# A message-passing layer: destination terms made window by window on the core instead of read back from a table in memory

## The chip, the cores and the metric

The kernel runs on one core of one Trainium2 chip. The core has a matrix engine (TensorE, PE in the profile, its weight loads PEld), a vector engine (VectorE, DVE), an activation engine (ScalarE, ACT), a programmable engine (GpSimd, POOL) and a queue engine that here only starts transfers (SyncE, SP). The metric is device microseconds for one execution, lower is better. "Group" below is 384 edges, "block" is four groups.

## The reference, cut to what matters

There are 12500 nodes with 64 features and 212500 edges with 32 features. The edges are sorted by destination.

```python
msg_in = concat([nodes[src], nodes[dst], edge_features])       # 212500 x 160
messages = relu(msg_in @ mW1 + mb1) @ mW2 + mb2                # hidden width 128
aggregated = segment_sum(messages, dst)                        # 12500 x 64
update = relu(concat([nodes, aggregated]) @ uW1 + ub1) @ uW2 + ub2
out = layernorm(nodes + update)
```

Since `mW1` acts on three parts, the hidden layer of an edge is a sum of three terms: source features, edge features, and a destination term `nodes[dst] @ mW1[64:128] + mb1` that depends on the destination alone.

## The kernel before, in words

All of it is float32. Edges go through in G = 554 groups of three tiles of 128 edges. The order of each engine's instructions is the order in which the program writes them (`manual_schedule`); the framework adds the semaphores. Because the edges are sorted, the destinations of one group lie within a window of W = 32 nodes that begins at the group's first destination. A flag checks on the chip that this holds; another routine (`unordered`, untouched, not run here) stands behind it.

What is kept on the core: `xc`, 65 partitions by 12544 columns (row 0 counts the edges of each node, rows 1 to 64 are the node features, transposed), and `agg`, the sum of hidden vectors by node.

For iteration g the main loop (L402 to L416) writes this:

- `inputs` (L257), every fourth group: SP loads the edge features of four groups into `st`.
- `gather(g + 16)` (L93): three indirect transfers by GpSimd, each 128 rows of source features, into one of 18 buffers `s`. The buffer of group g + 16 is that of group g - 2, so the gather waits until `sums(g - 2)` has read it.
- `tables_for(g + 8)` (L191): when its time has come, one `table()` (L180): up to four products of 128 columns of `xc` with `w1b` (the destination part of `mW1` and `mb1`) on PE, one ScalarE copy from PSUM, and one transfer of 256 KB to the table `by_dst` in memory. There are 25 of these.
- `window(g + 4)` (L269): SP reads 32 rows of `by_dst` from the group's first destination into the top 32 rows of `wm`, one of six right-hand sides of 128 x 128; the rest of `wm` holds the source and edge parts of `mW1`, loaded once. Every fourth group it first loads four starting columns into registers of SP and DVE.
- `onehot(g + 2)` (L282): DVE writes the one-hot of each edge's place in the window beside the gathered features.
- `turn(g + 1)` (L290): PE transposes three tiles of one-hot and features into `xt`; ScalarE copies them into `st` and sums the one-hots into `counts`.
- `hidden(g)` (L302): PE multiplies three tiles of `st` by `wm` into `pre`; ScalarE takes the relu into `h`. The one-hot rows pick the destination term out of the window.
- `sums(g - 2)` (L317): PE transposes the counts and multiplies `h` by the one-hots into `sg`, one of two PSUM buffers; a product is written four times over so that it is wide enough.
- a step of a pending node update (L385), four steps for every 512 nodes.
- `add(g - 2)` (L328): DVE adds `sg` into the window's columns of `agg`, and the counts into row 0 of `xc`, at columns held in a register.

Each engine takes its own share of this list in order. So DVE's order is one-hot of g + 2, then the update's steps, then the two additions of g - 2; PE's is transposes of g + 1, products of g, sums of g - 2. PSUM's eight banks are all given out: one for the iota, one for tables and updates, two each for `xt`, `pre` and `sg`.

The start-up clamps the first destinations to a plan of which table chunks are ready (`bound`, two sets of some 25 small fills on DVE).

Of the kernel before, what the change touches and what calls it, by code (L numbers as in the profile page):

```python
# [10 lines left out]
F32 = mybir.dt.float32  # L11
BF16 = mybir.dt.bfloat16
I32 = mybir.dt.int32
AF = mybir.ActivationFunctionType
ALU = mybir.AluOpType
ET = mybir.EngineType
PSUM = bass.MemoryType.PSUM
DRAM = bass.MemoryType.DRAM

P = 128  # L20
N = 12500
E = 212500
D = 64
DE = 32
H = 128
# [3 lines left out]
W = 32  # L29
TG = 3  # L30
GE = TG * P
G = (E + GE - 1) // GE
SB = 4
AHEAD = 16
NEXT = 4
NT = (E + P - 1) // P
NP = N + 44
CH = 512
TIMES = 4
# [8 lines left out]
def plan():  # L48


    import math

    def node(g, sign):
        q = min(1.0, g * GE / E)
        return g * GE * N / E + sign * (6.0 * math.sqrt((E - N) * q * (1 - q)) * N / E + 6)

    chunks, b = [], 0
    for e in [c * CH for c in range(1, N // CH + 1)] + [N]:
        opens = next((g for g in range(G) if node(g, 1) + W >= b), G)
        closes = next((g for g in range(G) if node(g, -1) >= e), G)  # L60
        n = e - b
        chunks.append((b, *((P, n // P) if n % P == 0 else (n // 2, 2)), opens, closes))
        b = e
    return chunks


PLAN = plan()
# [3 lines left out]
def ordered(ctx: ExitStack, tc: tile.TileContext, a, ok):  # L71
# [3 lines left out]
    nc = tc.nc  # L75
    x, out = a["x"], a["out"]
    const = ctx.enter_context(tc.tile_pool(name="const", bufs=1))
    dram = ctx.enter_context(tc.tile_pool(name="dram", bufs=1, space=DRAM))
    gp = ctx.enter_context(tc.tile_pool(name="gather", bufs=AHEAD + 2))
    stp = ctx.enter_context(tc.tile_pool(name="st", bufs=3))  # L80
    bp = ctx.enter_context(tc.tile_pool(name="bout", bufs=2))
# [30 lines left out]
    ones = const.tile([P, P], F32, name="ones")  # L112
# [3 lines left out]
    zero = const.tile([W, H], F32, name="zero")  # L116
# [5 lines left out]
    xc = const.tile([D + 1, NP], F32, name="xc")  # L122
# [4 lines left out]
    nc.sync.dma_start(xc[0:1, :].rearrange("o (p n) -> o p n", p=P), ones[:, : NP // P])  # L127
    w1b = const.tile([D + 1, H], F32, name="w1b")
    nc.scalar.dma_start(w1b[0:1, :], a["mb1"][None, :])
    nc.scalar.dma_start(w1b[1 : D + 1, :], a["mW1"][D : 2 * D, :])  # L130
    cuts = [0, 3 * CH, 12 * CH, N]
# [3 lines left out]
    NW = 6  # L135
# [9 lines left out]

    lo, hi = np.zeros(G), np.full(G, float(N - 1))
    for base, p, n, opens, closes in PLAN:
        lo[closes:] = base + p * n
        hi[:opens] = np.minimum(hi[:opens], base - W)

    def steps(v):

        at = [0, *(np.flatnonzero(np.diff(v)) + 1).tolist(), len(v)]
        return [(i, j, float(v[i])) for i, j in zip(at, at[1:])]

    bound = temp.tile([1, G], F32, name="bound")

    def set_bound(v):
        for i, j, value in steps(v):
            nc.vector.memset(bound[:, i:j], value)  # L160

    set_bound(hi)
    start_f = temp.tile([1, G], F32, name="start_f")
    nc.vector.tensor_scalar(start_f, first_f[0:1, :], 0.0, None, ALU.max)
    nc.vector.tensor_tensor(start_f, start_f, bound, ALU.min)
# [8 lines left out]


    by_dst = dram.tile([N + W, H], F32, name="by_dst")
    nc.sync.dma_start(by_dst[N:, :], zero)
    tables = list(PLAN)

    def table():  # L180
        base, p, n, _, _ = tables.pop(0)
        ps = ups.tile([H, CH], F32, name="u_ps").rearrange("p (n h) -> p n h", n=4)
        for k in range(n):
            nc.tensor.matmul(ps[:p, k], xc[:, base + k : base + p * n : n], w1b,  # L184
                             start=True, stop=True)
        t = bp.tile([P, 4, H], F32, name="t")
        nc.scalar.activation(t[:p, :n], ps[:p, :n], AF.Copy)  # L187
        nc.scalar.dma_start(
            by_dst[base : base + p * n, :].rearrange("(p n) h -> p n h", p=p), t[:p, :n])

    def tables_for(g):  # L191

        while tables and tables[0][3] <= g:
            table()

    SOON = NEXT + 4
    tables_for(SOON)


# [17 lines left out]
    nc.tensor.matmul(wps[:, 2, 0:1], u1s, b2, start=True, stop=True)  # L217
# [3 lines left out]

    nc.vector.tensor_tensor(ub1, ub1, wps[:, 2, 0:1], ALU.subtract)
# [8 lines left out]
    wrong = temp.tile([1, 2, G], F32, name="wrong")  # L231
    nc.vector.tensor_tensor(wrong[:, 0], first_f[0:1, :], bound, ALU.is_gt)
    set_bound(lo)
    nc.vector.tensor_tensor(wrong[:, 1], first_f[0:1, :], bound, ALU.is_lt)
    nwrong = temp.tile([1, 1], F32, name="nwrong")
    nc.vector.tensor_reduce(nwrong, wrong, mybir.AxisListType.XY, ALU.add)
# [18 lines left out]
    st, starts, hs = {}, {}, {}  # L255
# [13 lines left out]
    def window(g):  # L269
        if g >= G:  # L270
            return
        if g % SB == 0:
            n = min(SB, G - g)
            _, v = nc.values_load_multi_w_load_instructions(
                start_i[0:1, g : g + n], engines=[ET.SP, ET.DVE], min_val=0, max_val=N - 1,
                skip_runtime_bounds_check_because="they were clamped to the nodes on the chip",
            )
            for i in range(n):
                starts[g + i] = v[i]
        nc.sync.dma_start(wm[g % NW][:W, :], by_dst[bass.ds(starts[g], W), :])  # L280

# [35 lines left out]
    def sums(g):  # L317
        h, s = hs.pop(g), gathered.pop(g)
        sizes = tiles_of(g)
        sg = sgp.tile([P, TIMES + 1, W], F32, name="sg")  # L320
        nc.tensor.transpose(sg[0:1, TIMES, :], counts[:W, g : g + 1], ident[:W, :W])  # L321
        for j, p in enumerate(sizes):
            nc.tensor.matmul(sg[:, :TIMES, :], h[:p, j, :],  # L323
                             s[:p, j, :W].unsqueeze(1).to_broadcast([p, TIMES, W]),
                             start=j == 0, stop=j == len(sizes) - 1)
        return sg
# [6 lines left out]
    def update(base, p, n):  # L333
# [8 lines left out]
        def first(xin):  # L342
            u_ps = ups.tile([H, CH], F32, name="u_ps")
            nc.tensor.matmul(u_ps[:, :q], wc, agg[:, rows], start=True, stop=False)  # L344
            nc.tensor.matmul(u_ps[:, :q], ux, xc[:, rows], start=False, stop=True)  # L345
            u = up.tile([H, CH], F32, name="u")
            nc.scalar.activation(u[:, :q], u_ps[:, :q], AF.Relu, bias=ub1)
            nc.vector.tensor_tensor(xin[:p, :n], xin[:p, :n],
                                    u2b[:p].unsqueeze(1).to_broadcast([p, n, D]), ALU.add)
            return xin, u  # L350
# [31 lines left out]
    waiting = [(closes, update(base, p, n)) for base, p, n, _, closes in PLAN]  # L382
# [14 lines left out]
    for g in range(NEXT):  # L397
        window(g)
# [3 lines left out]
    for g in range(G + 2):  # L402
        if g < G:
            if g % SB == 0:
                inputs(g // SB + 2)
            if g + AHEAD < G:
                gather(g + AHEAD)
            tables_for(g + SOON)
            window(g + NEXT)
            onehot(g + 2)  # L410
            turn(g + 1)
            hidden(g)
        if g > 1:
            sg = sums(g - 2)
            step_update(g - 2)
            add(g - 2, sg)  # L416
# [331 lines left out]
```

## Time and profile before

| | |
|---|---|
| median of three runs | 2540.38 us (2536.92 to 2542.14) |
| the profiled execution, its time | 2528.93 us |
| its span, first to last instruction | 2527.2 us |
| PE, PEld busy | 1697.3 us (67%), 1457.9 us (58%) |
| POOL busy | 1570.3 us (62%) |
| ACT, DVE busy | 598.2 us (24%), 392.9 us (16%) |
| mean granted clock of TensorE | 0.786 |
| transfers from `by_dst`, to `by_dst` | 554 of 16 KB on SP's queue, 25 on ACT's |

The profile shows one execution. A line of groups reads: source line, engine, operation, output and inputs by the program's names, shape, count; then busy time and the mean of one in nanoseconds; then the idle time of that engine just before them and what ended most of it. In the timeline the columns are start and duration in microseconds, the engine, the line, the operation, its tiles, how many were merged, and in square brackets the idle time before it with what ended it. "remote" is a wait whose end the profile can't lay to an instruction. Ends of matmuls are modelled, so the better sign that a product is finished is the moment at which an engine that was waiting for it starts.

### The profile page before, as it was taken

To read this page: it belongs to the slowest core of one execution; us is meant where nothing else is said; L and a number is where in the kernel's file an instruction comes from. 1 tells how busy PE (TensorE), PEld (TensorE's weight loads), DVE (VectorE), ACT (ScalarE), POOL (GpSimd) and SP (SyncE) were. 2 spreads that over 40 slices of the span, in tenths; PEclk is the share of its full clock that TensorE was granted. 3 is DMA by queue.
4 is the path that set the end of the run, shared out by engine and by line. 5 is a ranking of instruction groups with operands and counts; after the bars stand their busy time and mean duration, and the time that the engine had idled before them with its cause. 6 is when DMAs were issued, how large, how long until landed. Compare 5 with 4: busy or idle time off the path is not lost.

```text
span 2527.2 us, 31410 instructions
## 1 busy us (share of the span) xinstructions
PE 1697.3 (67%) x9359; PEld 1457.9 (58%) x9359; DVE 392.9 (16%) x2103; ACT 598.2 (24%) x1740; POOL 1570.3 (62%) x1668
## 2 busy tenths in 40 slices
PE   0566767776676776776666766666667676677667
PEld 0455656665565665665555655556566565666556
DVE  3111111111111111111111111111111111111112
ACT  0222222222222222222222222222222222222223
POOL 6666666666666666666666665666666666666661
PEclk9787777777778677777877787788787778787879
DMA  5111111111111111111111111111111111111111
GB/s 127 34 43 46 40 43 45 41 44 43 40 44 41 42 47 39 45 43 40 43 41 42 47 42 40 40 43 44 41 42 47 36 47 40 43 47 38 46 39 28
DMA packets 99895, 111.48 MB, mean 44 GB/s; under 512 B 39997, under 2 KB 65062, under 8 KB 99590
## 3 DMA queue, kind: packets, MB, share of 16 engines
q0 software_dynamic: 53152, 54.51, 9.6%
q1 hardware_dynamic: 41928, 45.07, 6.4%
q10 hardware_dynamic: 4638, 9.80, 1.3%
q8 instruction: 79, 1.29, 0.2%
q14 instruction: 98, 0.80, 0.1%
HBM read 99.55 MB, written 9.62 MB: 43 GB/s over the span
## 4 chain that ended last, share of the span: by engine, by line
PE 66%; another core or an unknown queue 16%; issue 12%; DVE 2%; ACT 1%; DVEq 0%; DMA 0%; ACTq 0%
PE sg L323 25%; PE pre L307 21%; PE xt L298 12%; PE sg L321 2%; PE u_ps L184 2%; PE u_ps L357 2%; PE u_ps L344 1%; PE u_ps L345 1%; ACT st L299 1%; DVE o L374 0%; DVE mv L364 0%; DVE stats L363 0%; DVE xc L331 0%; DVE y L359 0%
## 5 line engine op out<-in xcount | busy, mean ns | idle before, releaser
L97 POOL DMA_INDIRECT s<-in_x,src_sb x1661 | 1569.6, 945 | 910.3 <-issue 420.5
L307 PE MATMUL pre<-wm,st 128*128 128x128 f32 x3322 | 635.3, 343 | 205.1 <-issue 140.3
L307 PEld LDWEIGHTS pre<-wm,st 128*128 128x128 f32 x3322 | 572.1, 254 | 241.7 <-issue 165.3
L323 PE MATMUL sg<-s,h 128*128 128x128 f32 x3322 | 660.4, 348 | 1.8 <-issue 1.8
L298 PE MATMUL xt<-ident,s 128*96 128x128 f32 x1661 | 355.4, 335 | 443.8 <-remote 246.7
L323 PEld LDWEIGHTS sg<-s,h 128*128 128x128 f32 x3322 | 535.6, 240 | 29.2 <-issue 1.7
L298 PEld LDWEIGHTS xt<-ident,s 128*96 128x96 f32 x1661 | 234.3, 159 | 501.7 <-remote 259.2
L299 ACT ACTIVATE st<-xt 96x384 f32<-96x384 f32 x554 | 267.9, 484 | 1002.3 <-PE xt L298 469.4
L311 ACT ACTIVATE h<-pre 128x384 f32<-128x384 f32 x553 | 268.8, 486 | 668.0 <-PE pre L307 257.3
L330 DVE TENSOR_TENSOR agg<-sg,agg 128x32 f32 x554 | 106.2, 192 | 1899.2 <-PE sg L323 761.2
L285 DVE TENSOR_TENSOR s<-iota,dlc 128x96 f32<-128x96 f32 x554 | 141.9, 257 | 54.6 <-issue 53.7
L184 PE MATMUL u_ps<-w1b,xc 65*128 65x128 f32 (+1 forms) x196 | 54.2, 453 | 112.9 <-DVE xc L331 80.3
L184 PEld LDWEIGHTS u_ps<-w1b,xc 65*128 65x128 f32 (+1 forms) x196 | 47.5, 326 | 118.2 <-issue 51.9
L321 PE MATMUL sg<-ident,counts 32*1 32x32 f32 x554 | 107.2, 194 | 0.0
L299 ACT ACTIVATION_READ_ACCUMULATOR st<-xt 96x1 f32 x554 | 106.0, 191 | 0.0
L331 DVE TENSOR_TENSOR xc<-sg,xc 1x32 f32 x554 | 99.2, 179 | 13.9 <-PE u_ps L345 5.3
L321 PEld LDWEIGHTS sg<-ident,counts 32*1 32x1 f32 x554 | 41.1, 74 | 90.2 <-issue 43.9
L357 PE MATMUL u_ps<-u,u 128*128 128x64 f32 (+1 forms) x196 | 49.5, 399 | 20.5 <-issue 11.2
L357 PEld LDWEIGHTS u_ps<-u,u 128*128 128x128 f32 (+1 forms) x196 | 47.1, 324 | 23.2 <-issue 12.2
L344 PE MATMUL u_ps<-agg,wc 128*128 128x512 f32 (+1 forms) x50 | 33.3, 753 | 18.0 <-DVE agg L330 12.2
L187 ACT ACTIVATE t<-u_ps 128x512 f32<-128x512 f32 (+1 forms) x25 | 14.7, 588 | 91.3 <-issue 43.7
L366 ACT ACTIVATE rstd<-mv,eps 128x4 f32<-128x4 f32 (+1 forms) x25 | 7.4, 297 | 103.8 <-DVE mv L364 42.1
(51 smaller groups left out, 188.1 us busy)
## 6 DMA issues: line engine op xcount, KB each, us to landing
s<-in_x,src_sb POOLq DMA_INDIRECT x1661
st<-in_efT SPq DMA_DIRECT2D x138, 192.0 KB
wm<-by_dst SPq DMA_DIRECT2D x554, 16.0 KB
by_dst<-t ACTq DMA_DIRECT2D x24, 256.0 KB
xin<-in_x SPq DMA_DIRECT2D x24, 128.0 KB
out<-o SPq DMA_DIRECT2D x24, 128.0 KB
xc<-in_xT ACTq DMA_DIRECT2D x1, 1589.0 KB
xc<-in_xT ACTq DMA_DIRECT2D x1, 1152.0 KB
```

The lines of the kernel that those rows point to most:

```text
L97: nc.gpsimd.indirect_dma_start(out=s[:p, j, W:], out_offset=None, in_=x[:, :], in_offset=bass.IndirectOffsetOnAxis(ap=src_sb[:p, t : t + 1 ...
L184: nc.tensor.matmul(ps[:p, k], xc[:, base + k : base + p * n : n], w1b, start=True, stop=True)
L285: nc.vector.tensor_tensor(gathered[g][:, :, :W], iota.unsqueeze(1).to_broadcast([P, TG, W]), dlc[:, g * TG : (g + 1) * TG].unsqueeze(2).to ...
L298: nc.tensor.transpose(xt[:, j * P : j * P + p], s[:p, j, :], ident[:p, :p])
L299: nc.scalar.activation(t[: D + W, c : c + n], xt[:, :n], AF.Copy, accum_out=counts[:, g : g + 1])
L307: nc.tensor.matmul(pre[:p, j, :], t[:, c + j * P : c + j * P + p], wm[g % NW], start=True, stop=True)
L311: nc.scalar.activation(h, pre, AF.Relu)
L321: nc.tensor.transpose(sg[0:1, TIMES, :], counts[:W, g : g + 1], ident[:W, :W])
L323: nc.tensor.matmul(sg[:, :TIMES, :], h[:p, j, :], s[:p, j, :W].unsqueeze(1).to_broadcast([p, TIMES, W]), start=j == 0, stop=j == len(sizes ...
L330: nc.vector.tensor_tensor(agg[:, at], sg[:, 0, :], agg[:, at], ALU.add)
L331: nc.vector.tensor_tensor(xc[0:1, at], sg[0:1, TIMES, :], xc[0:1, at], ALU.add)
L357: nc.tensor.matmul(o_ps[:p, k], u[:, k:q:n], u2, start=True, stop=True)
```

## The change

The table `by_dst`, its products, its copies and its transfers are gone, and with them the plan of ready chunks. `xc` gets a row of ones (row 65), so that `mb1` is its last row in `w1b`; row 0, the counts, meets a row of zeros. Once per block, `places` (written at iterations 1, 5, 9, ...) loads the four starting columns into DVE's registers and copies four windows of 66 partitions by 32 columns out of `xc` into `xw`, side by side. `windows` (written inside `sums` of the first group of a block, that is at iterations 2, 6, 10, ...) makes one product on PE, 128 window rows by 128, for the next block; it goes into 128 more columns of the same PSUM tile `sg` into which that `sums` then writes, and DVE copies its four parts of 32 rows by 128 columns into the top rows of four of now eight `wm`. Everything else in the loop stays.

```diff
-    xc = const.tile([D + 1, NP], F32, name="xc")
+    xc = const.tile([D + 2, NP], F32, name="xc")
+    nc.vector.memset(xc[:, N:], 0.0)
...
-    nc.sync.dma_start(xc[0:1, :].rearrange("o (p n) -> o p n", p=P), ones[:, : NP // P])
+    nc.sync.dma_start(xc[0:1, :].rearrange("o (p n) -> o p n", p=P), zero)
+    nc.sync.dma_start(xc[D + 1 :, :].rearrange("o (p n) -> o p n", p=P), ones[:, : NP // P])
...
-    NW = 6
+    NW = 2 * SB
...
-    def table():
-        base, p, n, _, _ = tables.pop(0)
-        ps = ups.tile([H, CH], F32, name="u_ps").rearrange("p (n h) -> p n h", n=4)
-        for k in range(n):
-            nc.tensor.matmul(ps[:p, k], xc[:, base + k : base + p * n : n], w1b,
-                             start=True, stop=True)
-        t = bp.tile([P, 4, H], F32, name="t")
-        nc.scalar.activation(t[:p, :n], ps[:p, :n], AF.Copy)
-        nc.scalar.dma_start(
-            by_dst[base : base + p * n, :].rearrange("(p n) h -> p n h", p=p), t[:p, :n])
...
-    def window(g):
...
-        nc.sync.dma_start(wm[g % NW][:W, :], by_dst[bass.ds(starts[g], W), :])
+    def places(b):
+
+        g, n = b * SB, min(SB, G - b * SB)
+        if n <= 0:
             return
+        _, v = nc.values_load_multi_w_load_instructions(
+            start_i[0:1, g : g + n], engines=[ET.DVE], min_val=0, max_val=N - 1,
+            skip_runtime_bounds_check_because="they were clamped to the nodes on the chip",
+        )
+        xw = xwp.tile([D + 2, SB, W], F32, name="xw")
+        for i in range(n):
+            starts[g + i] = v[i]
+            nc.vector.tensor_copy(xw[:, i, :], xc[:, bass.ds(v[i], W)])
+        xws[b] = xw, n
+
+    def windows(b, wp):
+
+        if b not in xws:
+            return
+        xw, n = xws.pop(b)
+        nc.tensor.matmul(wp[: n * W, :], xw[:, :n, :], w1b, start=True, stop=True)
+        for i in range(n):
+            nc.vector.tensor_copy(wm[(b * SB + i) % NW][:W, :], wp[i * W : (i + 1) * W, :])
...
     def sums(g):
...
-        sg = sgp.tile([P, TIMES + 1, W], F32, name="sg")
+        sgw = sgp.tile([P, (TIMES + 1) * W + H], F32, name="sg")
+        sg = sgw[:, : (TIMES + 1) * W].rearrange("p (t w) -> p t w", w=W)
+        if g % SB == 0:
+            windows(g // SB + 1, sgw[:, (TIMES + 1) * W :])
...
-    for g in range(NEXT):
-        window(g)
+    places(0)
+    windows(0, ups.tile([H, CH], F32, name="u_ps")[:, :H])
...
-            tables_for(g + SOON)
-            window(g + NEXT)
+            if g % SB == 1:
+                places(g // SB + 1)
             onehot(g + 2)
             turn(g + 1)
             hidden(g)
```

## The prediction

> **What bounds the kernel now.** I read the table of engines first, and it does not settle it: PE is busy 67% of the span and POOL 62%. The groups by line and POOL's waits settle it.
>
> ```profile
> L97 POOL DMA_INDIRECT s<-in_x,src_sb x1661 | 1569.6, 945 | 910.3 <-issue 420.5
> ```
>
> ```profile
> POOL s L97 <- issue: 420.5, 1376, 0.6
> POOL s L97 <- DVE agg L330: 301.7, 152, 8.2
> POOL s L97 <- remote: 68.6, 38, 2.6
> POOL s L97 <- PE sg L323: 59.9, 40, 3.1
> POOL s L97 <- PE pre L307: 25.2, 27, 4.3
> POOL s L97 <- PE xt L298: 17.9, 13, 3.6
> ```
>
> The gathers take 1569.6 us busy and 910.3 us of idle time before them, 2480 us of a span of 2527 us: POOL is never long without a gather, and what follows its last one is 47 us. A gather takes 0.945 us and 0.31 us (420.5 / 1376) to the next, so 1.25 us, 3.75 us for a group's three, 15.0 us for a block. The rest are pauses in which the next buffer is not yet read out: the last five rows, 473 us in 270 pauses, 1.75 us each, one for every 2.05 groups, 3.4 us in each of 139 blocks.
>
> Two stretches of the timeline say why it pauses although PE is not full. First with gathers running:
>
> ```profile
> 1203.77 0.50 PE L298 MATMUL xt<-ident,s 128*96 128x128 f32 x3 [1.03 <-PE sg L323]
> 1204.99 0.94 PE L323 MATMUL sg<-s,h 128*128 128x128 f32 x6
> 1206.01 0.94 POOL L97 DMA_INDIRECT s<-in_x,src_sb  x1 [0.31 <-issue]
> 1208.86 0.49 ACT L311 ACTIVATE h<-pre 128x384 f32<-128x384 f32 x1 [5.04 <-remote]
> 1208.88 0.19 DVE L330 TENSOR_TENSOR agg<-sg,agg 128x32 f32 x1 [5.22 <-remote]
> 1209.12 0.94 POOL L97 DMA_INDIRECT s<-in_x,src_sb  x1 [2.17 <-remote]
> 1209.25 0.48 ACT L299 ACTIVATE st<-xt 96x384 f32<-96x384 f32 x1
> 1209.37 0.19 DVE L330 TENSOR_TENSOR agg<-sg,agg 128x32 f32 x1
> ```
>
> PE's transposes and sums are over by 1205.9 by its own rows, but ScalarE, DVE and POOL, all idle, only learn of it at 1208.8, all at once, about 1.9 us after the last gather's row ended (1206.95). Then the end, when POOL has no more gathers:
>
> ```profile
> 2487.23 0.19 DVE L330 TENSOR_TENSOR agg<-sg,agg 128x32 f32 x1 [1.45 <-PE sg L323]
> 2489.21 0.19 DVE L330 TENSOR_TENSOR agg<-sg,agg 128x32 f32 x1 [1.46 <-PE sg L323]
> 2491.18 0.19 DVE L330 TENSOR_TENSOR agg<-sg,agg 128x32 f32 x1 [1.45 <-PE sg L323]
> ```
>
> Now a group takes 1.98 us and answers come at once. So PE could go at twice the pace; while gathers run, word of its finished products reaches the others late, mostly in bursts when POOL stops. The kernel lives with this because PE runs about two groups ahead without an answer: transposes of g + 2 need only a one-hot that stands behind the additions of g - 3. I can't say from the trace what holds the answers back; the rest uses only that they are late while POOL works.
>
> **What goes away.** Tables: 98 float32 products (196 rows of L184, 54.2 us busy together, 112.9 us idle before them, 80.3 of it for DVE's `xc` L331), 25 copies on ScalarE (14.7 us) and 25 ACT issues. Most that can be had is 54.2 + 112.9 = 167 us, least nothing. Of POOL's time only the pauses, 473 of 2480 us or 19%, wait on PE and DVE; I take that share: 0.19 x 167 = -32 us. The 554 window reads on SP, with the register loads there, lie beside all this: SP computes nothing, and PE's wait for them costs a sequencer slot; taken at nothing, hidden by the same 1.25 us pace of the gathers; without that cover PE would gain from 0 to the 140.3 us that L307 sat idle for "issue". The edge features on SP get earlier, and nobody waits for them. In the start-up the fills of `bound` are replaced by like ones, and one small product (L217) and one subtraction (L222, 0.13 us) go. Two more pairs of `wm` loads (0.3 to 2.1 us of SP issue each) and the row of ones stand ahead of the second half of the source indices, first needed by gather 49 near 72 us, and in the old order issued at 29.5 us. `places(0)` and its product come just before the first transposes: +2 us, bounds 0 and 5.
>
> **What PE gets.** 139 window products of 66 rows by 128 by 128. Nearest row L184: 54.2 / 98 = 0.55 us, 77 us together. PE has room (1.98 of 4.5 us a group), so by itself 0.19 x 77 = 15 us; I count it inside the trip below.
>
> **What DVE gets.** Per block four copies from PSUM. Nearest rows L219 and L220: 0.29 and 0.27 us, starts 0.21 us apart, so 3 x 0.21 + 0.27 = 0.90 us (1.16 if they don't overlap, 0.5 at the 0.13 us step of L330 to L331). And four copies of 32 columns inside SBUF at a register's address, no such row; L331, also 32 columns at a register, 0.13 us from start to start: 0.52 us, bounds 0.24 (four of L115's 0.06) and 1.76 (four of L167's 0.44 for 554 columns). The register load (L274, 0.35 us) moves by one iteration and stays one per block. These stand ahead of a one-hot, with the next transposes behind; 139 x 0.52 = 72 us, 19% of it on the pace: +14 us, bounds 0 and 245.
>
> **The new wait.** The product for the next block lies in `sums(4k)`. Its answer must come to DVE, DVE makes its four copies, and only then may `sums(4k)` write the PSUM tile that they read. Behind that on PE are the sums of 4k, the transposes of 4k + 4 and all later work; behind the copies on DVE, the additions of 4k and the one-hot of 4k + 5; and POOL waits for `sums(4k)` to get its buffer. Here PE can't run two groups ahead: it stands until its own late answer has come. The whole trip is 0.55 (product) + 0.90 (copies) + 0.94 (sums, L323's row at 1204.99) = 2.39 us. Least price: nothing, if the answer comes in the middle of a run of gathers. Most: each block pays a further pause and the whole trip in it, 139 x (1.75 + 2.39) = 575 us. I take the case between: with a pause each 2.05 groups and a stop at one fixed place in four, half of the stops fall together with one that PE makes anyhow, the other half cut a run of two groups in two, and cost one more pause with the copies inside it: 139 x 0.5 x (1.75 + 0.90) = +184 us.
>
> The Trainium skill ("PSUM — Partial Sum Buffer", section "PSUM bank collisions raise a hardware error") speaks against the change: two engines must be kept apart by semaphores on a whole bank and quadrant, not by address, so that copies and sums of one tile, in other columns, may not overlap. No run here shows a collision; without the rule's wait the sum would lack its 184 us.
>
> **GpSimd and DVE.** The new copies inside SBUF can hold up gathers. At the start long DVE operations inside SBUF meet gathers:
>
> ```profile
> 9.90 1.24 DVE L169 CAST dlc<-dlc_i 128x1662 f32<-128x1662 int32 x1 [0.57 <-issue]
> 10.60 1.35 POOL L97 DMA_INDIRECT s<-in_x,src_sb  x1 [0.30 <-issue]
> 11.18 1.89 DVE L170 TENSOR_TENSOR dlc<-dlc,first_f 128x1662 f32<-128x1662 f32 x1
> 12.26 1.63 POOL L97 DMA_INDIRECT s<-in_x,src_sb  x1 [0.30 <-issue]
> ```
>
> The two gathers take 1.35 and 1.63 us in place of 0.94: 1.10 us lost beside 3.13 us of DVE work, a third. In the loop DVE's operations read PSUM for one input and the gathers keep their 0.945 us. So 139 x 0.52 / 3 = +24 us straight on the pace, bounds 0 and 72.
>
> The skill ("SBUF — State Buffer", "Who interferes with whom") makes this an exclusive lock of the port that DVE's float32 copies in SBUF share with GpSimd: the loser waits for the whole instruction, with some 115 ns after it. By that, an estimate from the page, every copy that meets a gather would cost up to its length and 0.115 us, 139 x 4 x (0.13 + 0.115) = 136 us; the trace's third is what I use.
>
> **Sum.** 2529 - 32 + 2 + 14 + 184 + 24 = 2721 us for an execution like the profiled one, +192 us. That execution (2528.93) is 11 us below the median of the runs; on the median's scale 2540 + 192 = **2732 us**. Own range: from the trip at a quarter of the blocks' half price (92 us) to every block paying its pause and copies (368): 2640 to 2916.
>
> **Rivals.**
> 1. *The trip hides (faster).* The answer to the product comes while POOL still has gathers to do. For it: a run of two groups lasts 7.5 us, the trip 2.39; some answers do come in mid-run. Against it: the waits of 5.04 and 5.22 us above, with three things queued ahead of the answer. Then 2540 - 32 (or, with the chain's 2% for L184, -51) + 2 + 14 = 2524 to 2505 us, the lock adding nothing; I put it at 2512. It is also the case in which the program lets sums and copies overlap. It decides when the pauses stay at or below 270.
> 2. *The full price (slower still).* Each block pays a pause and the whole trip: 2540 + 575 + 8 = 3123 us. For it: after the burst POOL starts at once, so the product's answer is late nearly every time. Against it: half the stops coincide with old ones. Its sign is 400 pauses or more.
> 3. *PE is the bound.* Then only PE's work counts: 77 - 54 = +23 us, 2563. Against it: 1.98 us a group at the end.
> 4. *Gain and loss cancel* near 2540: a trip mostly hidden, copies that hold up the gathers.
>
> **Chances.** Forecast 0.62, first rival 0.21, second 0.11, third 0.02, fourth 0.04. The likeliest gives 2732. The range runs from 2490 (the first rival with a little more of the tables' 167 us) to 2960 (the forecast's end with the higher bounds of the copies); it leaves out the second rival and the outermost of the others. A measurement of this kernel tells about 0.2% (5 us) from no change. Slower 0.62 + 0.11 + 0.02 = 0.75; same 0.04; faster 0.21.
>
> **What would show it.** In the changed profile: no rows for the table and none for `by_dst`; POOL's idle time before L97 up by about 190 us, with more pauses (some 340) or longer ones; gathers above 945 ns by about 15; a new wait on PE ahead of the counts' transpose in every fourth group, ended by DVE's copies from `sg`; DVE's copies idle before for PE's window product, by microseconds. The pace of 1.25 us a gather inside a run should stay. Wrong if pauses fall, if PE does not stand before `sums(4k)`, or if the end of the kernel, without gathers, is where time goes.

## The result and the profile after

| | before | changed |
|---|---|---|
| median of four runs each, same chip | 2538.65 us (2534.01 to 2542.14) | 2654.02 us (2645.15 to 2672.06) |
| ratio, 95% interval | | 1.047, 1.0446 to 1.0494 |
| the profiled execution's span | 2527.2 us | 2670.3 us |
| mean granted clock of TensorE | 0.786 | 0.754 |

The change makes the kernel slower, by 115 us between the medians. The forecast was slower by 192 us: 2732 us, with a range from 2490 to 2960. The profiled execution of the changed kernel is the longest of its four, 18 us above their median, so differences between the two traces (143 us of span) are somewhat larger than those between medians.

The groups by line of the changed kernel (line, engine, operation, tiles, count; busy time and mean of one in ns; idle time before them and what ended most of it) show the gathers, the new wait on PE, DVE's additions, and the three new kinds of work:

```profile
L94 POOL DMA_INDIRECT s<-in_x,src_sb x1661 | 1575.2, 948 | 1039.4 <-DVE agg L301 444.3
L292 PE MATMUL sg<-ident,counts 32*1 32x32 f32 x554 | 107.5, 194 | 703.2 <-DVE wm L248 655.2
L301 DVE TENSOR_TENSOR agg<-sg,agg 128x32 f32 x554 | 106.3, 192 | 1496.4 <-PE sg L294 661.1
L248 DVE COPY wm<-sg 32x128 f32<-32x128 f32 x550 | 156.0, 284 | 352.6 <-remote 293.8
L238 DVE COPY xw<-xc 66x32 f32 x554 | 79.0, 223 | 48.7 <-DVE xc L302 26.3
L246 PE MATMUL sg<-w1b,xw 66*128 66x128 f32 (+1 forms) x276 | 66.7, 332 | 0.0
```

The gathers themselves are as they were (948 ns for 945, 5.6 us over all of them); the time is in the idle stretches before them, 1039.4 us in place of 910.3. The second row is the stop that the prediction was about: the counts' transpose, the first instruction of `sums`, waits 655 us for DVE's copies of the window product out of the same PSUM tile. It stands at all 138 of these places, 703 us in all. No such wait is in the trace of before, where the row is

```profile
L321 PE MATMUL sg<-ident,counts 32*1 32x32 f32 x554 | 107.2, 194 | 0.0
```

POOL's waits in the changed kernel (us in total, times, longest) say where that goes; "answer" here and below is the word to a waiting engine that PE's product is done:

```profile
POOL s L94 <- DVE agg L301: 444.3, 174, 9.0
POOL s L94 <- issue: 407.6, 1307, 3.7
POOL s L94 <- PE sg L294: 90.7, 52, 5.4
POOL s L94 <- remote: 31.0, 46, 2.8
POOL s L94 <- PE xt L266: 23.4, 21, 3.1
POOL s L94 <- PE pre L275: 15.9, 19, 1.7
```

The pace inside a run of gathers stayed (407.6 / 1307 = 0.31 us between two). What grew is the first row, the waits that end with the additions behind the sums: 301.7 us in 152 waits before, 444.3 in 174 now.

The granted clock does not explain the difference, although it is lower in the changed kernel: among the versions below, e3's profiled execution shows 0.803 and takes 2655 us, and e6's shows 0.744 and takes 2634 us.

One stop, in the timeline of the changed kernel (start and duration in us, engine, line, operation, tiles, idle time and what ended it):

```profile
1205.36 0.53 DVE L238 COPY xw<-xc 66x32 f32 x4 [0.37 <-DVE xc L302]
...
1205.68 0.94 PE L294 MATMUL sg<-s,h 128*128 128x128 f32 x6
...
1207.60 0.39 PE L246 MATMUL sg<-w1b,xw 66*128 66x128 f32 x2
...
1214.09 0.94 POOL L94 DMA_INDIRECT s<-in_x,src_sb  x1 [0.30 <-issue]
1217.01 1.18 DVE L248 COPY wm<-sg 32x128 f32<-32x128 f32 x4 [5.21 <-remote]
1217.03 0.49 ACT L279 ACTIVATE h<-pre 128x384 f32<-128x384 f32 x1 [3.75 <-remote]
1218.24 0.07 PEld L292 LDWEIGHTS sg<-ident,counts 32*1 32x1 f32 x1 [10.44 <-DVE wm L248]
1218.24 0.21 PE L292 MATMUL sg<-ident,counts 32*1 32x32 f32 x1 [10.25 <-DVE wm L248]
1218.38 1.35 PEld L294 LDWEIGHTS sg<-s,h 128*128 128x128 f32 x6
1218.38 1.65 PE L294 MATMUL sg<-s,h 128*128 128x128 f32 x6
1220.06 0.19 DVE L301 TENSOR_TENSOR agg<-sg,agg 128x32 f32 x1 [1.88 <-PE sg L294]
1220.30 0.95 POOL L94 DMA_INDIRECT s<-in_x,src_sb  x1 [5.27 <-DVE agg L301]
```

By PE's own rows the window product is over at 1207.99. DVE, idle for the 5.21 us before, starts its copies at 1217.01, 9 us later and 2 us after POOL's last gather ended (1215.03); ScalarE gets an older answer at the same moment. Only then come the copies (1.18 us), the sums (1.65), and the buffer's release: POOL stands 5.27 us, of which the copies and the sums are a good half. The pause of the kernel before that the prediction shows lacks them, because its sums had been issued before the answers came (at 1204.99, the answers at 1208.8).

This stop is one of the long ones: over the 138 stops, the time from the end of the product's rows to the first copy has a median of 2.3 us and a mean of 3.9. The sums behind it are slow as well: these six products take 1.65 us, where those at 1205.68 in the same trace took 0.94; from the first start to the last, which are not modelled, it is 1.23 us for 0.66. It is so after every one of the 69 stops at which PE stood for 3.5 us or more, while behind the short stops of e9 below (1.31 us in the mean) the sums mostly take 0.94.

The end of the changed kernel, when POOL has no more gathers, shows DVE's additions of five groups:

```profile
2621.50 0.19 DVE L301 TENSOR_TENSOR agg<-sg,agg 128x32 f32 x1 [2.64 <-PE sg L294]
2623.48 0.19 DVE L301 TENSOR_TENSOR agg<-sg,agg 128x32 f32 x1 [1.46 <-PE sg L294]
...
2625.46 0.19 DVE L301 TENSOR_TENSOR agg<-sg,agg 128x32 f32 x1 [0.56 <-PE sg L294]
...
2626.68 1.18 DVE L248 COPY wm<-sg 32x128 f32<-32x128 f32 x4 [0.69 <-PE sg L246]
2629.00 0.19 DVE L301 TENSOR_TENSOR agg<-sg,agg 128x32 f32 x1 [1.14 <-PE sg L294]
...
2630.98 0.19 DVE L301 TENSOR_TENSOR agg<-sg,agg 128x32 f32 x1 [1.10 <-PE sg L294]
```

Groups without a window product still take 1.98 us; the one with it takes 3.54 (2625.46 to 2629.00). So where answers are prompt a stop costs 1.56 us.

### The profile page after: what moved, and what is told of

It reads as the page before. It is cut to its first block, busy times and chain, and to the rows that moved or that the text cites. A ratio compares the mean times of both kernels' runs of the same rounds, so it can differ in the third digit from the quotient of the medians.

```text
span 2670.3 us, 30613 instructions
## 1 busy us (share of the span) xinstructions
PE 1611.5 (60%) x9439; PEld 1403.9 (53%) x9439; DVE 609.5 (23%) x3185; ACT 590.7 (22%) x1715; POOL 1576.0 (59%) x1668
## 4 chain that ended last, share of the span: by engine, by line
PE 54%; another core or an unknown queue 25%; DVE 10%; issue 9%; DMA 1%; DVEq 1%; ACT 0%; SPq 0%; ACTq 0%
PE sg L294 23%; PE pre L275 15%; PE xt L266 8%; DVE wm L248 4%; PE sg L292 3%; PE u_ps L328 2%; DVE s L253 1%; PE sg L246 1%; PE u_ps L315 1%; DVE xc L302 1%; PE u_ps L316 1%; DVE xw L238 1%; DMA u1s<-in_uW 1%; DVE agg L301 1%
## 5 line engine op out<-in xcount | busy, mean ns | idle before, releaser
L94 POOL DMA_INDIRECT s<-in_x,src_sb x1661 | 1575.2, 948 | 1039.4 <-DVE agg L301 444.3
L275 PE MATMUL pre<-wm,st 128*128 128x128 f32 x3322 | 592.4, 327 | 83.8 <-issue 73.4
L275 PEld LDWEIGHTS pre<-wm,st 128*128 128x128 f32 x3322 | 534.9, 239 | 107.7 <-issue 90.6
L266 PE MATMUL xt<-ident,s 128*96 128x128 f32 x1661 | 340.2, 324 | 203.1 <-PE sg L294 86.6
L248 DVE COPY wm<-sg 32x128 f32<-32x128 f32 x550 | 156.0, 284 | 352.6 <-remote 293.8
L238 DVE COPY xw<-xc 66x32 f32 x554 | 79.0, 223 | 48.7 <-DVE xc L302 26.3
L246 PE MATMUL sg<-w1b,xw 66*128 66x128 f32 (+1 forms) x276 | 66.7, 332 | 0.0
L246 PEld LDWEIGHTS sg<-w1b,xw 66*128 66x128 f32 (+1 forms) x276 | 54.8, 246 | 0.1
L318 ACT ACTIVATE u<-u_ps,ub 128x512 f32<-128x512 f32 (+1 forms) x25 | 16.9, 677 | 91.7 <-PE u_ps L316 36.9
```

What stands on the lines that cost most here:

```text
L94: nc.gpsimd.indirect_dma_start(out=s[:p, j, W:], out_offset=None, in_=x[:, :], in_offset=bass.IndirectOffsetOnAxis(ap=src_sb[:p, t : t + 1 ...
L246: nc.tensor.matmul(wp[: n * W, :], xw[:, :n, :], w1b, start=True, stop=True)
L248: nc.vector.tensor_copy(wm[(b * SB + i) % NW][:W, :], wp[i * W : (i + 1) * W, :])
L266: nc.tensor.transpose(xt[:, j * P : j * P + p], s[:p, j, :], ident[:p, :p])
L275: nc.tensor.matmul(pre[:p, j, :], t[:, c + j * P : c + j * P + p], wm[g % NW], start=True, stop=True)
```

## The experiments

Each ran beside the kernel before on the same chip; ratios are to it, and "us" made from a ratio is the ratio times 2540. The table counts pauses in the profiled executions, worked out from the rows of the gathers: a pause is the idle time over 0.30 us before the first gather of a group (counted if over 0.3 us more), and its place is the number, modulo four, of the group whose sums free that buffer. The sums of 4k stand behind the stop. The count leaves out the ordinary steps of about 0.30 us that some rows of POOL's waits put down to another engine; so it is lower than a count of those rows.

| kernel | pauses, us in all | of these, behind the sums of 4k | of other groups |
|---|---|---|---|
| before | 233, 396 us | 48, 91 us (mean 1.90) | 185, 305 us |
| changed | 252, 526 us | 78, 277 us (mean 3.54) | 174, 249 us |
| tables left out (e4) | 234, 372 us | 46, 82 us | 188, 290 us |
| product in its own bank (e1) | 214, 382 us | 67, 106 us | 147, 276 us |
| product behind the sums (e2) | 197, 367 us | 48, 90 us | 149, 276 us |
| two stops a block (e3) | 246, 513 us | 67, 201 us; of 4k + 2: 66, 137 us | 113, 176 us |
| one copy in four (e5) | 216, 462 us | 56, 194 us | 160, 268 us |
| copies in SBUF three times (e6) | 279, 482 us | 65, 186 us | 214, 296 us |

### The window product in a bank of its own (e1_own_bank)

```diff
-        sgw = sgp.tile([P, (TIMES + 1) * W + H], F32, name="sg")
-        sg = sgw[:, : (TIMES + 1) * W].rearrange("p (t w) -> p t w", w=W)
+        sg = sgp.tile([P, TIMES + 1, W], F32, name="sg")
...
-            windows(g // SB + 1, sgw[:, (TIMES + 1) * W :])
+            windows(g // SB + 1, ups.tile([H, CH], F32, name="u_ps")[:, :H])
```

> The changed kernel, with the window product written into the PSUM bank of tables and updates instead of the tile of the sums, so that the sums need not wait for DVE's copies; product, copies and their order stay. Theory A (PE's stop before the sums, in the shared tile, is the cost): the wait of L292 on DVE's copies (655 us) is gone, pauses of GpSimd fall from 608 us to about 450, time about 2510 us (2480 to 2550), some 1% below before and 140 below the change. Theory B (DVE's 1.1 us of added copies per block, ahead of additions and one-hots, is the cost wherever the product lies): no less than 2620. Theory C (the copies hold up the gathers at the port that GpSimd and DVE share): no less than 2620, gathers' mean stays at 948 ns.

Measured: 2521.3 us (2515.57 to 2526.55), ratio 0.9901 (0.9883 to 0.992). The groups of this kernel:

```profile
L94 POOL DMA_INDIRECT s<-in_x,src_sb x1661 | 1575.0, 948 | 897.9 <-issue 404.7
L291 PE MATMUL sg<-ident,counts 32*1 32x32 f32 x554 | 107.3, 194 | 0.0
```

The same product, at the same place in the order, with the same copies, is now 0.99 of the time before and not 1.047 of it. The counts' transpose no longer waits at all. So the wait for the shared tile costs 1.047 - 0.990 = 0.057, 145 us, and everything else in the change together is a gain.

### The product behind the sums, in the same tile (e2_after_sums)

```diff
-        if g % SB == 0:
-            windows(g // SB + 1, sgw[:, (TIMES + 1) * W :])
         nc.tensor.transpose(sg[0:1, TIMES, :], counts[:W, g : g + 1], ident[:W, :W])
...
+        if g % SB == 0:
+            windows(g // SB + 1, sgw[:, (TIMES + 1) * W :])
         return sg
```

> The changed kernel, with the window product written after the sums of the same iteration, in the same PSUM tile; PE has nothing behind it that writes the tile for two groups. Theory A: the stop is gone, 2500 to 2560 us. Theory B: 2620 or more, since the copies still stand ahead of the additions on DVE, and the additions now wait for the product too.

Measured: 2509.88 us (2507.08 to 2511.59), ratio 0.9866 (0.985 to 0.9883). This is 1.3% less than the kernel before, and the fastest complete version on chips where that takes 2540 us. Its groups:

```profile
L94 POOL DMA_INDIRECT s<-in_x,src_sb x1661 | 1575.0, 948 | 880.5 <-issue 398.0
L290 PE MATMUL sg<-ident,counts 32*1 32x32 f32 x554 | 107.1, 193 | 0.0
L248 DVE COPY wm<-sg 32x128 f32<-32x128 f32 x550 | 156.4, 284 | 519.5 <-PE pre L275 147.7
```

The same instructions on the same tile, with the product written behind the sums: PE's wait is gone, DVE now waits instead (519.5 us before the copies), and PE's rows hold only 3.4 us of waiting for these copies. By the ratios the order is worth 1.047 - 0.9866 = 0.060, 153 us. In the table of pauses the profiled executions differ by 186 us behind the sums of 4k, and by 27 us the other way at the other groups. That a longer pause at the stop lets other answers come in would explain the 27 us; it was not tried apart.

### Two stops in each block (e3_two_stops)

```diff
-        g, n = b * SB, min(SB, G - b * SB)
+        g, n = b * 2, min(2, G - b * 2)
...
-        if g % SB == 0:
-            windows(g // SB + 1, sgw[:, (TIMES + 1) * W :])
+        if g % 2 == 0:
+            windows(g // 2 + 2, sgw[:, (TIMES + 1) * W :])
...
-            if g % SB == 1:
-                places(g // SB + 1)
+            if g % 2 == 1:
+                places(g // 2 + 2)
```

> The changed kernel, with a product for two windows every second group instead of one for four every fourth: 277 stops of PE instead of 139, the same number of copies. Theory A: the stop's share (115 us net, 147 with the tables' 32 us that it hides) doubles, less the shorter copies: 2740 to 2800 us. Theory B or C (DVE's copies themselves): the same copies, 2640 to 2670 us.

Measured: 2670.6 us (2655.37 to 2674.7), ratio 1.0501 (1.0481 to 1.0521). The groups of this kernel:

```profile
L292 PE MATMUL sg<-ident,counts 32*1 32x32 f32 x554 | 107.8, 195 | 809.9 <-DVE wm L248 541.2
```

The expected doubling did not come: 275 stops in the loop cost at most 19 us more than 138 (0.0031 of 2540 is 8 us; the intervals, 1.0446 to 1.0494 and 1.0481 to 1.0521, overlap). Two stops a block do not cost twice one. The time is at the edge of what theory B or C expected (to 2670), but e1 and e2 had already ruled these out, since they keep the copies and lose the price. The pauses at the first place shrink to 201 us from 277 in the changed kernel, those at the second grow to 137 from 55, those at odd groups fall to 176 us from 195 there and 206 before the change. This agrees with a PE that stops for late answers about every two groups anyhow, so that a forced stop mostly moves a pause; each stop here also has half of the copies.

### The tables alone taken away (e4_no_tables)

```diff
-        nc.sync.dma_start(wm[g % NW][:W, :], by_dst[bass.ds(starts[g], W), :])
+        nc.sync.dma_start(wm[g % NW][:W, :], a["efT"][:, bass.ds(starts[g], H)])
...
-            tables_for(g + SOON)
```

> The kernel before without the 24 tables made in the loop and at the start; the window reads take 32 rows of 512 bytes from the edge features in memory instead, so the destination term is left out of what is computed. What the tables cost. As forecast: 2540 - 32 = 2508 us (bounds 2373 to 2540). Rival (PE's room swallows them): 2535 to 2540.

Measured: 2509.98 us (2509.26 to 2511.7), ratio 0.9867 (0.985 to 0.9883): 35 us less than the 2544.75 of the kernel before beside it. The forecast's term for the tables was 32 us. The groups of this kernel:

```profile
L97 POOL DMA_INDIRECT s<-in_x,src_sb x1661 | 1575.7, 949 | 885.6 <-issue 410.6
```

A gather takes 949 ns here, where DVE has no copies of windows at all; so the 948 ns of the changed kernel are not made by them. And since e2 comes out equal (0.9866 to 0.9867), the new product and the eight new copies a block cost nothing that shows, as long as no one waits for them. This is net of one thing that e4 keeps and e2 has not, the 554 window reads; what these alone cost was not tried.

### One copy out of PSUM where there were four (e5_one_copy)

```diff
-        for i in range(n):
+        for i in range(1):
             nc.vector.tensor_copy(wm[(b * SB + i) % NW][:W, :], wp[i * W : (i + 1) * W, :])
```

> The changed kernel with one of the four copies from PSUM per stop; the destination term of three groups in four is left out of what is computed (zeros). What the copies are worth inside the stop. Theory A (the stop is a trip PE, DVE, PE that stands in GpSimd's pauses; in the changed kernel 78 of 139 blocks pause at that place): about 0.75 us less in each of 78 to 139 trips, 2654 - 58 to - 105 = 2550 to 2596 us. Rival (only the late answer to the product costs, the copies run beside it): 2640 to 2660.

Measured: 2615.38 us (2610.3 to 2619.56), ratio 1.0303 (1.0286 to 1.032). Against the change that is 0.0167, 42 us, for 138 x (1.18 - 0.28) = 124 us less of copying: about a third of it. That lies between what the two theories expected. The price of the stop has two parts, then: a smaller one that goes with three of the four copies, and a larger one that is there with a single short copy. The late answer to the product is the likely cause of the larger one, and the slow sums behind a long stand may add to it; no run takes either away alone. In the table the pauses behind the sums of 4k keep a mean of 3.46 us but are 56 in place of 78.

### The copies inside SBUF three times (e6_xw_thrice)

```diff
-            nc.vector.tensor_copy(xw[:, i, :], xc[:, bass.ds(v[i], W)])
+            for _ in range(3):
+                nc.vector.tensor_copy(xw[:, i, :], xc[:, bass.ds(v[i], W)])
```

> The changed kernel with each of the 554 window copies inside SBUF written three times, the same result: 1108 copies more. Forecast's terms: 8 x 0.18 us more per block ahead of a one-hot, 19% of it on the pace, +38 us, and a third of it held up at the port, +67 us: 2690 to 2760. Rival (no price for such small copies): gathers stay at 948 ns, 2650 to 2670 us.

Measured: 2630.92 us (2605.89 to 2635.58), ratio 1.0327 (1.0272 to 1.0383). The groups of this kernel:

```profile
L94 POOL DMA_INDIRECT s<-in_x,src_sb x1661 | 1575.6, 949 | 996.9 <-issue 408.4
L239 DVE COPY xw<-xc 66x32 f32 x1662 | 311.1, 210 | 112.6 <-DVE xc L303 32.5
L293 PE MATMUL sg<-ident,counts 32*1 32x32 f32 x554 | 107.6, 194 | 377.1 <-DVE wm L249 279.9
```

232 us more of DVE work inside SBUF, ahead of every fourth one-hot, and the kernel is not slower; the gathers take 949 ns for 948. With that the port that DVE and GpSimd share falls as a cost. The copies ahead of the one-hot show none either; here alone something else might make up for it, but e2 and e4 come out equal with and without these copies. The time lies below both expectations, and it is even less than that of the change, by 0.0143 or 36 us, with no overlap of the intervals. Why a later one-hot helps is open; the stop's pauses are fewer (65 in place of 78), and PE stands there for 377 us in place of 703.

### Plain transfers in place of the gathers (e7 to e10)

In the kernel before, by GpSimd (e7) and by SP (e8); in the changed kernel, by GpSimd (e9); and in the version with the product behind the sums, by GpSimd (e10):

```diff
-            nc.gpsimd.indirect_dma_start(
-                out=s[:p, j, W:], out_offset=None, in_=x[:, :],
-                in_offset=bass.IndirectOffsetOnAxis(ap=src_sb[:p, t : t + 1], axis=0),
-            )
+            r = (t * 97) % (N - P)
+            nc.gpsimd.dma_start(s[:p, j, W:], x[r : r + p, :])
```

> The kernel before with each indirect gather replaced by a plain transfer of 128 consecutive rows of the node features, issued by GpSimd too: other source features are computed with. Is it the gather that holds PE's answers back? If it is the indirect form alone: answers at once, a group near 2 us or near three times the time of one issue on GpSimd. If any transfer from GpSimd's queue does it: pauses of about 2 us between runs as before.

> The same plain transfers issued by SP; GpSimd has nothing to do in the loop. Other source features are computed with. If GpSimd's work holds the answers back: ScalarE and DVE start at once after PE's rows, about 2 us a group, 1200 to 1500 us in all. If the traffic into SBUF does it: answers as late as before, 2000 us or more.

> The changed kernel with the plain transfers of 128 consecutive rows from GpSimd in place of the gathers (other source features are computed with), beside 1374 us for the kernel before with the same transfers. Answers are prompt there and PE is the bound. Theory A (a stop is a trip PE, DVE, PE of at least product, four copies and two answers, late or not): 1374 - 54 (tables) + 77 (products) + 139 x 1.5 = about 1600 us. Rival (all of the price comes from late answers, so that none is left): 1380 to 1420 us.

> The kernel with the product after the sums, with the same plain transfers. No stop: 1374 - 54 + 77 = about 1400 us in either theory; what e9 has more than this is the stop with prompt answers.

Measured, one execution of each: 1373.79 us (e7) and 1486.21 us (e8), where the kernel before took 2541.02 us beside them; 1517.03 us (e9) and 1309.16 us (e10), in a batch in which it took 2108.48 us (more of that below). The engines of e7, and DVE's additions in its timeline:

```profile
PE 1268.2 (92%) x9359; PEld 1142.7 (83%) x9359; DVE 393.2 (29%) x2103; ACT 620.6 (45%) x1740; POOL 878.4 (64%) x1668
```

```profile
700.28 0.19 DVE L328 TENSOR_TENSOR agg<-sg,agg 128x32 f32 x1 [1.04 <-PE sg L321]
...
702.26 0.19 DVE L328 TENSOR_TENSOR agg<-sg,agg 128x32 f32 x1 [1.46 <-PE sg L321]
...
704.24 0.19 DVE L328 TENSOR_TENSOR agg<-sg,agg 128x32 f32 x1 [1.46 <-PE sg L321]
```

With the same number of transfers of the same size, GpSimd's queue among them (1661 of 0.535 us), the answers of PE are prompt and a group takes 1.98 us in the middle of the kernel. Over the whole execution, the time from the end of a group's sums on PE's rows to DVE's addition has a median of 0.04 us here and of 3.17 us in the kernel before. So neither a busy GpSimd nor the traffic of 32 KB a transfer is enough to delay the answers; in this batch, in which the kernel before took 2536 to 2543 us in all of its seven runs, they are late with the gathers and prompt without. The 128 scattered rows and the indirect form were not tried apart, and e11 and e12 below show that gathers alone are not enough either.

e9 and e10 differ only in the order that e2 changed. The wait in e9, then one stop in its timeline:

```profile
PE sg L290 <- DVE wm L246: 181.3, 138, 2.3
```

```profile
699.87 0.39 PE L244 MATMUL sg<-w1b,xw 66*128 66x128 f32 x2
...
700.29 1.18 DVE L246 COPY wm<-sg 32x128 f32<-32x128 f32 x4 [0.69 <-PE sg L244]
701.53 0.07 PEld L290 LDWEIGHTS sg<-ident,counts 32*1 32x1 f32 x1 [1.46 <-DVE wm L246]
```

Here PE stops at every block (138 times), for copies that start at once, and the stops cost 1517.03 - 1309.16 = 208 us, 1.50 us each. Of this 181 us (1.31 a stop) are the wait itself; PE's busy time is 31 us longer too (1258.5 for 1227.5 us, at a granted clock of 0.975 for 0.996). Both absolute times were lower than expected; the difference is what the expectation of 1.5 us a stop said, and the rival, that no price is left, is out.

### The product behind the sums, and each one-hot one group earlier (e11, e12)

```diff
-            onehot(g + 2)
+            onehot(g + 3)
```

> The kernel with the product after the sums (2510 us), with gathers again, and the one-hot of g + 3 instead of g + 2 in iteration g, so that PE's transposes no longer hang on the additions just before. If PE's run-ahead is bounded by that one-hot, as the prediction says, GpSimd's runs get longer and its pauses fewer: 2400 to 2480 us. Rival (the answers that ScalarE needs bound it): 2500 to 2515 us.

> The same kernel as in the run before it: window product and copies behind the sums, and each one-hot written one iteration earlier, so that PE's transposes of g + 2 need an answer that is one group older. Where TensorE's answers come late while gathers run (the kernel before at about 2540 us): the theory that a run of gathers ends when PE runs out of work that it may do without an answer expects longer runs and fewer pauses, some 160 in place of 197, about 300 us of them in place of 368, and 2440 us, ratio 0.95 to 0.975 to the kernel before. The rival, that a run ends for the gathers' own buffers alone (18, three to a group, each free only by its group's sums), expects the time of the version without the earlier one-hot, ratio 0.983 to 0.99. Where answers are prompt (the kernel before near 2108 us) both expect a ratio of 1.00, as GpSimd's gathers follow each other without a pause.

Measured: 2108.01 us, ratio 0.9996 (0.9986 to 1.0005), and again 2107.64 us, ratio 0.9998 (0.9988 to 1.0007). In both batches the kernel before itself took 2108 us (13 runs each, 2106.0 to 2111.82), not 2540. The question, whether an earlier one-hot makes the runs of gathers longer, could not be answered there, since the runs have no end. POOL's waits of e12:

```profile
POOL s L94 <- issue: 361.7, 1187, 0.3
POOL s L94 <- DMA s<-in_x,src_sb: 75.7, 227, 3.0
```

and one group of its timeline:

```profile
1205.57 0.86 PE L275 MATMUL pre<-wm,st 128*128 128x128 f32 x6
...
1206.52 0.49 ACT L279 ACTIVATE h<-pre 128x384 f32<-128x384 f32 x1 [0.18 <-PE pre L275]
```

ScalarE learns of PE's product at once, with the same gathers running, and POOL has no pause at all by the count of the table: its gathers follow each other 0.30 us apart, and PE waits for them instead (506.8 us). There 1661 x 1.25 = 2076 us of gathers are the whole time.

## Why the prediction was right in direction and too large

*The bound.* "GpSimd's gathers set the pace, and they pause for PE's late answers" held in every run with gathers in the batches that gave 2540 us. e7 shows the cause of the lateness from one side: without gathers it is gone. The prediction's 270 pauses, one for every 2.05 groups, are too many: those rows hold steps of 0.30 us too, and the table has 233, one for every 2.4 groups.

*The tables, -32 us.* Measured -35 us (e4). Taking the pauses' share of PE's time, 19%, came close here. That it is the right weight is not shown: the same 19% gave `places` a price that is not there.

*The window product and the start-up, inside the trip and +2.* e2 minus e4 is zero within their intervals (0.0017 or 4 us each side), net of the window reads that e2 has not; the 77 us estimated for the product were 66.7 us, hidden.

*`places` ahead of the one-hot, +14 us.* Not there. The copies took 79.0 us (72 were estimated), but e2 with them equals e4 without, and three times as much did no harm (e6). The step that failed is "19% of it on the pace": DVE idles over 1496 us ahead of its additions alone, so the one-hot probably had time to spare.

*The shared port, +24 us.* Not there: 948 ns a gather with the copies, 949 with three times as many (e6) and 949 without any (e4). The row it was taken from was real but other work, operations of 1.24 and 1.89 us over 1662 columns; nothing of it carried to copies of 0.13 to 0.22 us. The Trainium skill ("SBUF — State Buffer", section "Who interferes with whom") made it 136 us by the estimate in the prediction; the runs show none of it. The page lets a copy lock the port only when its operands meet the conditions of a mode, and no run tells whether these copies did.

*The new wait, +184 us.* The mechanism is as described: PE stands before `sums(4k)` (655 us), for copies that stand for a late answer, and POOL's buffer is late behind it. The Trainium skill's rule ("PSUM — Partial Sum Buffer", section "PSUM bank collisions raise a hardware error"), that two engines are kept apart in a bank by semaphores whatever the addresses, agrees with this: the copies read other columns of the tile than the sums write, and PE waited for them all the same. It is a wait of the program's semaphores, so the runs do not show what would happen without it. The size was 145 us (e1) to 153 us (e2). At its own place the sum was nearly exact against e2: 186 us in the profiled execution, 1.35 us a block, where 1.32 was forecast; 27 us of it came back at the other groups, and the profiled execution is 18 us above the median.

That closeness is partly luck, because the sum behind the number was half wrong. The forecast let half of the stops, 70, add a pause of 1.75 us and copies of 0.90, and put the other half, which fall together with pauses that are there anyhow, at nothing. By the table 30 pauses came on top at this place, 78 for 48, at 3.54 us each: 106 us. The other 48 were not free but grew from 1.88 to 3.54 us: 80 us. Copies and sums now stand inside them, and both took longer than the forecast had them: four copies 1.18 us for 0.90, the sums 1.65 us (the median of the stops) for 0.94. That PE's products run slower after a long stand was not in the prediction at all. In all there are 252 pauses for 233, where some 340 for 270 were forecast; by the rows that the forecast counted it is 312, but in that count e2, which has no stop, has 317. e3 confirms that stops do not add up by number.

*The sum.* -35 for the tables, nothing for product, copies and port, +145 to +153 for the stop: +110 to +118 us, against 115 measured. The forecast of +192 exceeds it by the two terms that are not there (38 us) and by the stop (31 to 39). With e2 the sum closes of itself, since its terms are steps from one version to the next; the independent one is e1, which leaves 9 us more than e2 unexplained.

*The rivals.* That the trip hides is refuted by PE's 655 us and by the time; the sign it named, pauses at or below 270, can't tell, as the two counts differ (252 by the table, 312 by the rows). The full price is refuted by either count, where 400 was its sign, and by the time; PE as the bound by e1, with the same work on PE and 2521 us. That gain and loss cancel near 2540 did not come either. Still open is why e6 is faster than the change, what the larger part of the stop's price consists of, and what ends a run of gathers.

## What to carry to other kernels

Work added in front of a chain is cheap by its own duration and dear by what it makes wait: the same product and copies cost some 150 us ahead of the sums and nothing that shows behind them. So move the reader of a shared PSUM tile behind the tile's other writer, or give it a bank. Do not price a forced stop by the number of stops alone: twice as many cost at most 19 us more here, and pauses that were there anyhow grew too, because work was left to do inside them when the late answer came. A share of busy time that is far from full on every engine (PE 67%, POOL 62%) is a reason to look at one late answer in the timeline before pricing anything.

## What the runs showed of the hardware that was not expected

The delay of PE's answers goes with the gathers: 4.56 us a group with 1661 of them (2527 / 554), of which 3.75 are the gathers' own pace, and 1.98 us with plain transfers of the same size from the same queue. An answer came 3.17 us late in the median with the ones and 0.04 us with the others.

The delay is not always there. The same kernel before took 2534 to 2549 us in three batches of runs and 2106 to 2112 in the two last. The runs name chip 0 (e1 to e4) and chip 9 (e5 to e8) with 2540 us, and chip 9 (e9 to e11) and chip 1 (e12) with 2108, so the chip's number alone doesn't tell them apart. Both batches with 2108 us hold the version with the earlier one-hot; whether that, other work on the chip, or the chip itself decides it stays open. The trace's ends of matmuls are modelled, so it cannot say either whether the products end late or only the word of it. The granted clock is 0.78 in the one and 0.90 in the other, which is too little for the 9 us of the stretch shown. With the prompt answers of e12 the median from the sums to the addition is 0.04 us, with the same gathers.

A stop costs less where answers are late (145 to 153 us) than where they are prompt and PE is the bound (208 us), perhaps since some of the late ones fall together with pauses that are there anyhow. What the change costs with gathers and prompt answers was not tried. PE waits 506.8 us for gathers in e12, and the stops cost 208 us in e9: by an estimate from these two it would cost little.
